# The opening of an eight-block attention and FFN kernel: statistics reordered, one head corrected on TensorE, three heads left to the quartets

## The chip, the cores and the metric

The kernel is one program on one core of a Trainium2 chip. Five engines work side by side, each on its own list of instructions in a fixed order: TensorE (PE in the profile), VectorE (DVE), ScalarE (ACT), GpSimd (POOL) and SyncE (SP), which issues DMAs. An instruction starts when its own engine has come to it and the semaphores that it names have been counted up by others. The metric is the device time of one execution in microseconds, as the median of several runs. All times below are microseconds unless marked otherwise.

## The reference, cut to what matters

The reference is a chain of eight residual blocks on an input of 2 sequences of 512 rows and 512 columns (that is what the kernel reads; it is held as eight tiles of 128 rows by 512 columns, four to a sequence). Each block takes the rows, normalises each of them, computes an attention or an FFN, and adds the result to the rows. The change touches only the first block, a latent attention with 32 heads:

```python
xn = (x - mean(x)) / sqrt(var(x) + 1e-5)        # row by row
C_q = xn @ Wq_d + bq_d                          # 12 columns
C_kv = xn @ Wkv_d + bkv_d                       # 4 columns
q = (C_q @ W_qk + b_qk)                         # 32 heads of 4 columns
scores = q . C_kv / sqrt(4)                     # per head, all pairs of rows
out = softmax(scores) @ (C_kv @ Wv_u + bv_u)    # per head
x = x + out @ Wo + bo
```

The second block (an FFN with a low-rank adapter) begins inside the first one: its preparation and products for the first sequence are interleaved with the last part of the attention. Blocks three to eight follow and are the same instructions in the same order in both kernels.

## The kernel before, in words

The function `attn_latent_small` is the first block. Products in fp32 take TensorE several passes, so queries and keys are kept as two parts, a high part rounded to a shorter format and the rest. Packed side by side along the contraction, one fast product then gives nearly the fp32 result. The helper `halved` makes them: `top` is the high part (a product with a constant column, line 481), and line 482 adds it to the full value in the packed tile. It works on VectorE for the first sequence's keys and latent queries and on POOL for everything else.

**The opening.** PE runs 30 transposes of the identity (`warm`). Meanwhile the four row tiles of the first sequence arrive by DMA. VectorE takes statistics of a tile (`statistics`, lines 205, 207, 241), POOL the inverse root (line 243), and VectorE writes the centred rows `xn` (line 215). PE transposes `xn` (`place`, line 228) and ScalarE copies the result into the room of the transposed rows. This goes by pairs: statistics of tiles 0 and 1, centring of 0 and 1, then the same for 2 and 3. After each tile come 5 or 10 more `warm` transposes. Then VectorE prepares the packed query weights `wqks` (lines 787 and 788) and takes the statistics of the second sequence's four tiles; PE computes the latent queries and the latent keys of the first sequence (line 473, 4 fp32 products each), and VectorE evicts and packs them (lines 497 and 490, 481, 482).

**Heads.** There are 8 groups of 4 heads for each sequence, called t; `head(b, t)` makes the packed queries of one. It is a fast product (line 503), and then one of two ways. For heads 0 and 1 of the first sequence, ScalarE copies the high part (line 506), PE adds a correction into the same bank (`correct`, line 199), and ScalarE copies the bank to the packed queries (line 509). For all others, ScalarE copies the bank into a buffer `wv_diag` (line 513), and POOL makes both parts (lines 481 and 482). There is one buffer `wv_diag`, so the next such copy waits for POOL; it is used later for other things as well, as is the buffer `ctxT`.

**Quartets.** A quartet u (0 to 15) is one t of one sequence. For it there are 16 score products (line 589), each reduced on VectorE to the row maximum (line 597). POOL splits the maxima (lines 606 and 607). `maxima` transposes them on PE and corrects the packed queries by them (lines 615, 199, 618). Then the transposed scores (line 627) go through ScalarE's exponential (line 630), and PE multiplies them with the latent values (line 637). The work of neighbouring quartets overlaps: the loop has eight steps per quartet, and each issues two score products of the next quartet, two transposed products of this one, and on every second step the values of an earlier one. Scores and transposed scores have three PSUM banks each, the values have bank 6, and everything else has bank 7 alone, as long as the loop runs up to the last quartet.

**What fills the gaps.** A list `extra` holds pieces of other work as generators: the remaining heads, the transposes of the second sequence (`put`), its latents (`queries(1)`, `latents(1)`), the fold of two weights into one, the bias, and later the division, projection and FFN products of the first sequence. `slices(cost)` takes pieces from the front until their costs reach the given sum (a matmul, a put or a head is 1). Twelve steps ahead of the loop (`n` from 0 to 11) each issue two scores, a slice and two filler products (`fill`, line 758) that keep PE busy. In the loop, a step takes a slice when it has no values to do; the last quartet takes more. Where `extra` is empty at the start of a slice, three fills stand there instead. In these two loops PE's instructions stay in the order in which the program issues them; the other engines' order is chosen by a scheduler. In the opening both PE and VectorE keep the program's order.

When the values of the last quartet of a group of four are done, `following(u)` gives further pieces, which are put at the end of `extra`. Behind the loop, what is left in `extra` is run.

## Time and profile before

| quantity | value |
|---|---|
| median of three runs | 1962.3 (1960.98 to 1963.4) |
| time of the profiled execution | 1963.88 |
| its span, first to last instruction | 1962.2 |
| mean granted TensorE clock | 0.997 |
| PE busy | 1930.2 (98%) |
| VectorE busy | 1373.6 (70%) |
| POOL busy | 1020.8 (52%) |
| ScalarE busy | 937.7 (48%) |
| first row tile landed | 3.42 |
| query products start | 12.12 |
| first score product | 23.36 |
| quartet loop starts | 42.04 |
| last quartet's steps start | 234.81 |
| its raw sums are transposed | 254.49 |

The span and the profiled execution's time differ by 1.7, what lies around the program. The profiled execution is 1.6 longer than the median. A PE that is busy for 98% sets the end almost everywhere, but ends of matmuls are modelled and neighbouring ones overlap, so the starts are what is read here. The rows of the first block are at the beginning; its last products are at about 262.

### The profile page before, as it was taken

What the parts mean: (1) busy time and instruction counts of PE and PEld (TensorE: products, weight loads), DVE (VectorE), ACT (ScalarE), POOL (GpSimd) and SP (SyncE); (2) the same over time, 40 slices, a digit from 0 to 9 for tenths busy, and PEclk for the clock granted to TensorE, in tenths of its full rate; (3) what the DMA queues carried; (4) which work ended last, traced back from release to release, by engine and by line L of the source; (5) the groups of instructions that cost most, each with busy time, mean ns of one, the idle gap of its engine ahead of it and who ended that gap; (6) DMA issues with size and microseconds to landing.
All of it is one profiled execution on the core that took longest, in us unless ns stands there. A gap on an engine that the chain in (4) does not pass through costs nothing.

```text
span 1962.2 us, 40652 instructions
## 1 busy us (share of the span) xinstructions
PE 1930.2 (98%) x15690; PEld 1201.3 (61%) x15690; DVE 1373.6 (70%) x3457; ACT 937.7 (48%) x2460; POOL 1020.8 (52%) x1112
## 2 busy tenths in 40 slices
PE   9999999999999999999999999999999999999999
PEld 5333356777777777777777545666565554654654
DVE  8889658767776676777765577777777755847853
ACT  3786624444444343444443167666666411641550
POOL 4331055776756667677763246565655546216221
PEclk9999999999999999999999999999999999999999
DMA  3010222322321322232223213020101002002001
GB/s 136 17 44 1 76 70 69 86 76 89 94 67 46 97 76 82 76 98 76 79 79 86 71 23 109 8 74 7 62 13 55 23 11 49 2 2 43 2 2 44
DMA packets 69296, 108.96 MB, mean 56 GB/s; under 512 B 13922, under 2 KB 48994, under 8 KB 62052
## 3 DMA queue, kind: packets, MB, share of 16 engines
q1 hardware_dynamic: 68804, 104.15, 18.2%
q8 instruction: 127, 2.08, 0.4%
q0 software_dynamic: 288, 2.10, 0.3%
q14 instruction: 77, 0.63, 0.1%
HBM read 80.00 MB, written 4.19 MB: 43 GB/s over the span
## 4 chain that ended last, share of the span: by engine, by line
PE 87%; POOL 5%; DVE 4%; issue 2%; ACT 1%; DMA 0%; SPq 0%; DVEq 0%; POOLq 0%; ACTq 0%
PE held L1022 13%; PE held L281 11%; PE held L1157 9%; PE held L190 9%; PE held L357 8%; PE held L637 3%; PE held L589 3%; PE held L1094 3%; PE held L473 2%; PE held L1516 2%; PE sc L190 2%; PE held L1513 1%; PE tp L1789 1%; PE held L1514 1%; PE sc L2109 1%
## 5 line engine op out<-in xcount | busy, mean ns | idle before, releaser
L302 ACT ACTIVATE room<-room,nmax 128x128 f32<-128x128 f32 (+3 forms) x384 | 212.6, 557 | 354.6 <-DVE nmax L292 352.4
L281 PE MATMUL held<-kT,q 128*32 128x32 f32 (+15 forms) x4096 | 264.2, 397 | 5.3 <-DVE invs L310 1.7
L292 DVE CUSTOM_DVE_ANT_0 room<-held,mask 128x128 f32<-128x128 f32 (+3 forms) x384 | 179.0, 487 | 63.3 <-PE held L281 57.9
L281 PEld LDWEIGHTS held<-kT,q 128*32 128x32 f32 x4096 | 143.4, 110 | 87.2 <-issue 38.0
L357 PE MATMUL held<-turned,vals 32*128 32x384 f32 (+7 forms) x2784 | 190.0, 416 | 0.5 <-issue 0.5
L597 DVE TENSOR_REDUCE nm<-held 128x1 f32<-128x512 f32 x256 | 161.2, 682 | 22.4 <-PE held L627 14.8
L357 PEld LDWEIGHTS held<-turned,vals 32*128 32x128 f32 (+1 forms) x2784 | 149.3, 167 | 39.2 <-issue 22.6
L315 ACT ACTIVATE room<-room,invs 128x128 f32<-128x128 f32 (+3 forms) x316 | 153.3, 551 | 41.9 <-DVE invs L310 41.7
L254 DVE TENSOR_TENSOR rows<-rows,held 128x512 f32<-128x512 f32 x198 | 129.5, 673 | 31.8 <-PE held L1022 31.3
L330 DVE STREAM_TRANSPOSE turned<-room 128x1152 f32<-128x1152 f32 x80 | 107.8, 1361 | 40.3 <-ACT room L315 21.6
L243 POOL TENSOR_TENSOR rstd<-ve,mhalf 128x1 f32<-128x1 f32 x64 | 36.2, 569 | 179.4 <-DVE ve L241 176.1
L1183 POOL TENSOR_TENSOR q<-q,room 128x256 f32<-128x256 f32 x64 | 45.3, 729 | 124.2 <-DVE q L1166 113.6
L1201 POOL TENSOR_TENSOR q<-q,cosq 128x512 f32<-128x512 f32 x60 | 88.0, 1467 | 31.6 <-DVE t L1198 31.6
L1157 PE MATMUL held<-room,w 128*128 128x256 f32 x384 | 95.0, 383 | 0.0
L1202 POOL TENSOR_TENSOR q<-q,t 128x512 f32<-128x512 f32 x64 | 86.7, 1355 | 6.3 <-DVE q L1201 2.5
L302 ACT ACTIVATE probs<-probs,nmax 128x128 f32<-128x128 f32 (+3 forms) x128 | 70.6, 553 | 37.8 <-DVE nmax L292 37.0
L1022 PE MATMUL held<-w,ctxT 128*128 128x256 f32 x360 | 86.5, 383 | 0.1
L589 PEld LDWEIGHTS held<-keys,qs 32*128 32x128 f32 x256 | 31.1, 181 | 85.4 <-DVE nm L597 58.9
L630 ACT ACTIVATE pt<-held 128x512 f32<-128x512 f32 x128 | 69.7, 599 | 26.1 <-PE held L627 20.7
L2123 POOL TENSOR_SCALAR_AFFINE_SELECT room<-room 128x512 f32<-128x512 f32 x32 | 20.3, 635 | 118.2 <-ACT room L2119 118.2
L1537 POOL TENSOR_TENSOR q<-t,t 64x512 f32<-64x512 f32 x62 | 78.9, 1272 | 4.9
L630 ACT ACTIVATE room<-held 128x512 f32<-128x512 f32 x128 | 69.6, 600 | 24.4 <-PE held L627 21.7
(441 smaller groups left out, 5005.1 us busy)
## 6 DMA issues: line engine op xcount, KB each, us to landing
w<-in_b_wq SPq DMA_DIRECT2D x16, 1024.0 KB, 4.9
w<-in_b_wo SPq DMA_DIRECT2D x16, 1024.0 KB, 5.8
vals<-v SPq DMA_DIRECT2D x256, 64.0 KB, 2.1
w<-in_m_wo SPq DMA_DIRECT2D x8, 1024.0 KB, 6.3
w<-in_b_wk SPq DMA_DIRECT2D x16, 256.0 KB, 2.8
w<-in_b_wupv SPq DMA_DIRECT2D x16, 256.0 KB, 2.6
w<-in_m_wqn SPq DMA_DIRECT2D x8, 384.0 KB, 3.6
rows<-in_x SPq DMA_DIRECT2D x8, 256.0 KB, 4.7
```

The costliest lines, as they stand in the source:

```text
L190: last = self.nc.tensor.matmul(out, lhsT, rhs, start=(i == 0), stop=(i == len(pairs) - 1))
L254: self.nc.vector.tensor_tensor(x, x, ps.rearrange("p (t d) -> p t d", t=2), op)
L281: nc.tensor.matmul(ps[32 * i : 32 * i + 32, a - lo : b - lo], q[:, at : at + 32], keys[:, a:b], start=True, stop=True,)
L292: nc.vector.tensor_tensor_reduce(out=row, in0=ps[:, :kv], in1=self.mask_back[:, :kv] if qt % 2 else self.mask[:, S - kv :], op0=ALU.add, o ...
L302: nc.scalar.activation(row, row, AF.Exp, bias=nmax, scale=-1.0, accum_out=total[:, qt : qt + 1])
L315: self.nc.scalar.activation(row, row, AF.Identity, scale=each)
L330: self.nc.vector.transpose(out[:, :last], probs[:, :last])
L357: self.nc.tensor.matmul(out[:, :, :n], values(i, j), rhs, start=(j == blocks[0]), stop=(j == stop[i]),)
L597: k.latest = nc.vector.tensor_reduce(nm[u % 2][:, qt, at : at + 1], ps, AX.X, ALU.max, negate=True).ins
L630: nc.scalar.activation(probs[u, kc][:, g], ps, AF.Exp)
L1022: k.nc.tensor.matmul(out, lhsT[:, i, bass.ts(t, P)], rhs[i], start=not (after or t or i), stop=i == 1, skip_group_check=True,)
L1157: nc.tensor.matmul(out, lhsT[:, c], rhs[:, c], start=c == 0, stop=c == 1)
```

## The change

It has five parts, all in `attn_latent_small`.

- *Row statistics in another order.* The statistics of tiles 0, 1 and 2 come first, then the centring of 0 and 1, then the statistics of 3, and the centring of 2 and 3. The transposes and `warm` products of PE keep their order. Of the second sequence's four statistics, the last stands behind the packing of the latent queries.
- *One head corrected on TensorE.* Only head 0 is made by correction, and it is made at once: its product, five transposes of the identity, the correction, five transposes, then two fills ahead of the first scores. Before, heads 0 and 1 were made with two fills, two corrections and four fills. The high part of the first sequence's keys (`latents(0)`) goes to the buffer `wv_diag` instead of the two buffers `high`.
- *Two buffers for the query products.* Odd t use `ctxT`, even t `wv_diag`. The tile of `halved` is kept to one buffer for tags other than `high`. The weights' fold, which writes `ctxT`, is made later by the scheduler.
- *Three heads left.* Heads 5, 6 and 7 of the first sequence leave the twelve steps and stand at the head of the loop's list; head 1 comes into the twelve steps. The steps 10 and 11 then find `extra` empty and take three fills each. Heads 5 to 7 count as light pieces (`light`), as the second sequence's heads do.
- *The division earlier.* For the first half of a sequence (`half == 0`), `following(u)`, which is one division, goes to the second place of `extra` instead of to its end.

By the built programs' order, PE gets ten more transposes and two more fills and loses one correction; VectorE's instructions are the same in number. The last pieces shift: the last quartet takes three more products of the FFN and no division of quartet 11, and one put and one centring stand behind the loop.

```diff
-            top = lp.tile(list(out.shape), F32R, tag=tag, name="high")
+            top = lp.tile(list(out.shape), F32R, tag=tag, name="high", bufs=1 if tag != "high" else None)
...
-            k.latest = halved(nc.gpsimd if b else nc.vector, keys[b], full, 0)
+            k.latest = halved(nc.gpsimd if b else nc.vector, keys[b], full, 0, "high" if b else "wv_diag")
...
-            if (b, t) < (0, 2):
+            if (b, t) == (0, 0):
...
-            full = one([P, S], "wv_diag")
+            full = one([P, S], "ctxT" if t % 2 else "wv_diag")
...
-                extra.extend(following(u))
+                at = len(extra) if half else 1
+                extra[at:at] = following(u)
...
-            for t in range(0, NT, 2):
-                pair = [k.statistics(t + i) for i in range(2)]
-                centred = [k.centred(t + i, known=pair[i]) for i in range(2)]
-                for i in range(2):
-                    k.place(t + i, centred[i], k.turn)
-                    k.warm(5 + 5 * i)
+            ahead = [k.statistics(t) for t in range(3)]
+            centred = [k.centred(t, known=ahead[t]) for t in range(2)]
+            ahead.append(k.statistics(3))
+            for t in range(NT):
+                if t == 2:
+                    centred += [k.centred(i, known=ahead[i]) for i in (2, 3)]
+                k.place(t, centred[t], k.turn)
+                k.warm(10 if t % 2 else 5)
...
-            known = {t: k.statistics(t) for t in range(NT, NTILES)}
-            run([queries(0), latents(0)])
+            known = {t: k.statistics(t) for t in range(NT, NTILES - 1)}
+            run([queries(0)])
+            known[NTILES - 1] = k.statistics(NTILES - 1)
+            run([latents(0)])
             first = k.latest
-            starts = [head(0, t) for t in range(2)]
-            for _ in range(3):
-                for piece in starts:
-                    next(piece, None)
-                fill(2, of_values)
-        extra = [centre(NT, NT + 1), head(0, 2), head(0, 3), put(NT), put(NT + 1)]
+            for _ in head(0, 0):
+                k.warm(5)
+            fill(2, of_values)
+        extra = [centre(NT, NT + 1), head(0, 1), head(0, 2), head(0, 3), put(NT), put(NT + 1)]
         extra += [centre(NT + 2, NT + 3), latent_values(0), head(0, 4), put(NT + 2)]
-        extra += [put(NT + 3), head(0, 5), head(0, 6), head(0, 7)]
-
+        extra += [put(NT + 3)]
+
+        others = [head(0, t) for t in range(5, 8)]
...
-        later = [queries(1), latents(1), *heads[:4], latent_values(1)]
+        later = [*others, queries(1), latents(1), *heads[:4], latent_values(1)]
...
-                    light = not extra or extra[0] in heads + adds
+                    light = not extra or extra[0] in others + heads + adds
```

## The prediction

> **What bounds the kernel.** I read the page first, then a table of stretches of the first stage, then the engines' rows in order of time and the chain inside it. Everything below is in the first 262 us: behind the last transposes of this stage the order of instructions on all five engines is the same in both kernels, so the other 1,700 us are taken as unchanged.
>
> The page of the profiled execution, span and busy shares:
> ```profile
> span 1962.2 us, 40652 instructions
> ...
> PE 1930.2 (98%) x15690; PEld 1201.3 (61%) x15690; DVE 1373.6 (70%) x3457; ACT 937.7 (48%) x2460; POOL 1020.8 (52%) x1112
> ```
> PE is hardly ever idle. So a matmul added costs its length, unless it falls into one of PE's waits; the waits are what has to be found. The stretches of the first stage (columns: length, then busy time and instructions of PE, weight load, DVE, ACT, POOL, the granted clock, DMA):
> ```profile
> 0.00:21.34 21.34, 17.68 (x95) 13.19 (x95) 15.44 (x37) 4.28 (x7) 10.35 (x25) 1.00 0.80 273
> 21.34:42.04 20.70, 20.14 (x87) 11.30 (x87) 18.09 (x39) 7.37 (x13) 10.03 (x12) 1.00 0.12 41
> 42.04:48.17 6.13, 6.13 (x25) 2.12 (x25) 5.45 (x10) 4.63 (x9) 2.25 (x3) 1.00 0.00 0
> ...
> 139.06:172.23 33.17, 31.54 (x195) 11.25 (x195) 30.96 (x57) 23.34 (x44) 4.86 (x9) 1.00 0.00 1
> ...
> 210.81:234.81 24.00, 24.00 (x139) 7.80 (x136) 16.09 (x28) 17.56 (x33) 1.42 (x5) 1.00 0.08 31
> 234.81:254.49 19.68, 18.97 (x94) 6.52 (x93) 7.60 (x17) 10.38 (x20) 1.65 (x3) 1.00 0.16 54
> ```
> The opening (to 21.34) has 3.7 us of PE idle, the last quartets (210.81 to 254.49) almost none: what moves there costs its full length. Four steps after 42.04 are PE's too. The chain of waits through the opening:
> ```profile
> 12.28 6.88 PE held L473 x16
> ...
> 20.50 0.70 DVE keys L482
> ...
> 21.34 0.71 PE held L758 x2
> 22.04 0.47 PE held L199 x2
> 22.51 0.92 PE held L758 x4
> 23.43 0.42 PE held L589
> ```
> Query and latent products, then the keys' two halves on DVE, then fills and corrections, then the first scores. VectorE's rows ahead of that, and the loads of row tiles 1 and 2 (SyncE, line 90):
> ```profile
> 5.46 0.54 DVE L215 TENSOR_SCALAR xn<-rows,ln_mv,rstd 128x512 f32<-128x512 f32 x1
> 6.45 0.55 DVE L215 TENSOR_SCALAR xn<-rows,ln_mv,rstd 128x512 f32<-128x512 f32 x1 [0.45 <-POOL rstd L243]
> 6.91 0.69 DVE L205 BATCH_NORM_STATS2 ln_stats<-rows 128x6 f32<-128x512 f32 x1
> ```
> ```profile
> L90 SPq DMA_DIRECT2D rows<-in_x x2: 417/424/432, 1.3 to 1.7; - x2
> ...
> DMA to landing us min/median/max: 3.0/3.7/4.4
> ```
> The second of these two loads is tile 2: issued at 1.7, landed 4.4 later, at about 6.13. Before, its statistics are asked for only at 6.91, so nobody waits.
>
> **The change, part by part.**
>
> *Row statistics.* Tile 2's statistics now stand ahead of the first centring in VectorE's order. They start at 6.15 (landing) instead of the centring's 5.46. One group (3.44 to 4.46) takes 1.02 in period, so xn0 starts at 7.16, ends at 7.71, and PE's first transposes start at 7.75, not 6.40. The wait for the square root (0.45) is filled, but it was not on PE's path. PE then has two rounds of 4 transposes, 5 warm ones, 4, 10, each 9.54 to 12.12 = 2.58 long: 7.75 + 5.16 = 12.91 for the query products, against 12.12. The later centrings are in time: xn1 8.2 for 8.7, xn2 9.6 for 10.3, xn3 (root at 10.05) 10.6 for 11.3. Cost +0.79. If the tile had landed by 5.46 it would be +0.1; if PE's clock falls in the wait, see the rivals.
>
> *One statistic moved behind the query product.* VectorE idles 0.84 before the latents' eviction (19.19), later 19.98; the group of 1.0 ends by about 19.5. Nothing; without that cover up to 0.5.
>
> *One head corrected on TensorE, its fills.* The keys follow the latents by the same 2.15, so the first fill starts at 21.34 + 0.79 = 22.13. From there to the first score stood two fills, two corrections, four fills (21.34 to 23.36, 2.02); two fills remain (0.54): first score 22.67. The single head's product, ten transposes (10 x 0.109; the chain has ten in 1.09), its correction and copies (0.59 each) run while PE would wait for the keys: the copy ends at 20.80, the last transposes by 21.6, before 22.13. The own buffer for the keys' high part ends a wait of ScalarE (1.3) that was beside. Gain 1.48 against 0.79: the scores start 0.69 earlier.
>
> *Twelve score steps.* Steps 0 to 8 hold the same four heads, four puts and latent values as before, in another order; head 1 with its two POOL operations (0.69 + 1.28) has the second buffer. Steps 9 to 11 lose two heads (0.43 each in the chain, at 23.86) and get six fills (0.235 each, by the chain's pairs of 0.47). Before, 37.68 to 42.04 = 4.36 was 3.56 of PE and 0.8 waits for VectorE (eight reductions of 0.61 and the coefficients). Now PE has 3 x 0.43 + 12 x 0.235 = 4.11; VectorE ends about then. I take 4.2, -0.15 (bounds -0.25 and +0.55: all hidden, none hidden). The quartet loop starts 0.84 earlier.
>
> *Three heads in the loop.* They take the first three slots, where fp32 products of 1.06 stood. A slot's head shares one bank (7) with the next, so the next product waits for ScalarE's copy, which queues behind two exponentials:
> ```profile
> L630 ACT ACTIVATE room<-held 128x512 f32<-128x512 f32 x128 | 69.6, 600 | 24.4 <-PE held L627 21.7 <-PE held L589 1.9
> ...
> L513 ACT COPY wv_diag<-held 128x512 f32<-128x512 f32 x14 | 8.3, 593 | 10.1 <-POOL qs L482 6.0 <-PE held L503 4.1
> ```
> In order of time two exponentials take 1.09 (not 2 x 0.6), so a step is 1.09 + 0.59 = 1.68 of ScalarE, against 0.86 of PE. Four steps: 0.62 to the first exponential, 3 x 1.68, 0.1, one product 1.06 = 6.82, against 6.13: +0.69. Bounds: PE alone 7 x 0.43 + 1.06 = 4.07 (-2.06), POOL's 2.05 per head 3 x 2.05 + 1.49 = 7.64 (+1.51). I take ScalarE's, since the four pairs of steps with a head from 91.02 to 102.10 last 2.77 each = 4 x 0.545 + 0.59, ScalarE's sum. The second buffer gives nothing there: of the 6.0 above, 5.6 lie in the opening, 0.4 in the loop.
>
> *The shift.* Every later piece comes three slots later. Slots are fixed in number, a heavy pair of steps lasts 2.93. Three query products come in at 2.93, three products of tile 1 leave for the last quartet at 2.92; the division of quartet 11 moves up (2.80) into the place of the one empty slot (141.07 to 143.92, 2.85). Sum 0, bounds -1.0 and +1.0: the 1.6 of PE idle in 139 to 172, where VectorE has 30.96 of 33.17.
>
> *The last quartet.* It takes three more products of 1.06 and loses a division's and a put's transposes (0.59 each): +2.0, PE is full there. The put now stands behind the loop, in PE's 0.71 wait for the copy of the raw sums: 0. The last centring is ready 4.7 us after the last step's start, its transposes are due at 5.2: no wait. Bounds +1.4 (half a product hidden) and +2.6 (put not covered).
>
> Sum: -0.69 - 0.15 + 0.69 + 0 + 2.0 = **+1.85 us**. A check by work: PE gets ten transposes (1.09) and two fills (0.47), loses a correction (0.24), +1.3; the rest is 2.8 more idle in the first steps less what the waits near 20, 40, 141 and 254 us give up.
>
> The profiled execution took 1963.88 us with a span of 1962.2; the median of three is 1962.3. On its own time the sum gives 1965.7; on the median **1964.1 us**, +0.09%. A measurement of this kernel tells about 0.2% (3.9 us) from no change, so this is no change.
>
> **The clock, row and rule.** PE is now idle from 6.4 to 7.75. The granted clock by stretches of 3.4 us:
> ```profile
> 18.44:21.85 3.41, 1.69 (x6) 0.86 (x5) 2.59 (x5) 1.15 (x2) 0.00 (x0) 1.00 0.93 378
> 1800.20:1803.60 3.40, 1.95 (x17) 1.23 (x16) 1.96 (x9) 0.00 (x0) 3.32 (x3) 1.00 0.63 104
> 1803.60:1807.00 3.40, 3.40 (x8) 1.18 (x4) 2.75 (x9) 0.00 (x0) 0.26 (x1) 0.50 0.46 75
> ```
> With 1.69 of PE busy in such a stretch the clock stayed, with 1.95 it was halved for the next. The stretch 4.78 to 8.20 will have about 2.1. So the rows allow either; halved, 3.41 us do half their work, 1.7 lost. [...]
>
> **The rivals.**
> - *The third tile decides (slower).* PE's idle grows with tile 2's landing; from 6.55 on (0.4 later than here) PE has about 1.7 or less in its stretch and I would expect the halved clock: 0.4 + 1.7 above my sum, 1966.2 and more. For it: the 4.4 us from issue to landing against 2.6 for tile 0. Against: the row at 18.44. The halved clock without a later landing gives 1965.8.
> - *The heads hide (faster than my sum).* If ScalarE's copies do not hold up PE, the first steps cost 4.07: -2.75, 1961.3. For it: ACT is busy 48%. Against: the single bank.
> - *The order of statistics does what it says.* Tile 2 landed by 5.46: 1963.4. Against: the landing row.
> - *A gain that shows* (under 1958.4) would need the heads hidden and the last quartet free as well: 1964.1 - 2.75 - 2.0 = 1959.3 is not there yet, and with the middle's -1.0 it just is.
>
> **Numbers.** My sum, with the order-of-statistics case, 0.59; the third tile and the clock 0.19, nearly all beyond 3.9 us or close below it; heads hidden 0.16; all hidden at once 0.05; not thought of 0.01. Faster by over 0.2%: 0.06; slower by over 0.2%: 0.18; same 0.76. Range: from 1960.0 (heads hidden and half the middle's bound) to 1967.0 (the third tile a little later still).
>
> **What would show it.** Right: VectorE's third statistics wait for a load at 5.5 to 6.1; the query products start at 12.9; first score 22.7; loop start 41.2; ScalarE without idle in the three following steps; 11 products of 1.06 in the last quartet. Wrong: a clock of 0.5 in 8.2 to 11.6; PE stalls at the maxima, because POOL's splits now stand behind other waiting operations of its queue; VectorE's reductions waiting between 139 and 172.

## The result, and the profile after

| | kernel before | changed kernel |
|---|---|---|
| median of 20 executions each, same chip | 1963.70 | 1968.68 |
| lowest and highest | 1960.68, 1966.06 | 1964.13, 1970.80 |
| profiled execution, its span | 1962.2 | 1968.7 |

The ratio is 1.0020 with a 95% interval of 1.0014 to 1.0026: the change makes the kernel 2.7 to 5.1 us slower. It goes by mean times, about 1967.8 against 1963.6; the median of the changed kernel lies 0.9 above its mean. The prediction said +1.85 us on 1962.3, thus 1964.1, and 1960.0 to 1967.0. So the sign of the sum was right and its size was not, and the base was too low as well: the median of three executions shown before was 1962.3, that of the 126 executions of the kernel before that came with all later runs is 1964.1.

The page of the changed kernel, span and busy shares:

```profile
span 1968.7 us, 40679 instructions
...
PE 1933.3 (98%) x15701; PEld 1203.2 (61%) x15701; DVE 1375.7 (70%) x3457; ACT 937.0 (48%) x2459; POOL 1022.3 (52%) x1114
```

PE has 3 us more to do, and the span is 6.5 longer. The stretches of the first stage (length, then busy time and instructions of PE, weight load, DVE, ACT, POOL, then the granted clock, the DMA share and GB/s): up to the first filler, up to the loop's start, the first four steps, the rest of quartet 0, and then four stretches of 3.41 us as the clock is granted:

```profile
0.00:22.09 22.09, 18.82 (x105) 14.19 (x105) 15.83 (x37) 4.80 (x7) 9.78 (x25) 1.00 0.78 268
22.09:41.87 19.78, 19.35 (x85) 10.92 (x85) 17.76 (x39) 5.28 (x9) 8.28 (x10) 1.00 0.12 38
41.87:49.08 7.21, 6.29 (x22) 2.27 (x21) 5.12 (x9) 5.64 (x11) 4.70 (x6) 0.74 0.00 0
49.08:57.16 8.08, 8.08 (x43) 2.50 (x43) 4.82 (x8) 4.62 (x9) 1.50 (x3) 0.81 0.01 2
38.57:41.98 3.41, 3.41 (x18) 2.01 (x16) 2.90 (x6) 0.00 (x0) 0.00 (x0) 1.00 0.00 0
41.98:45.39 3.41, 2.66 (x14) 1.08 (x14) 2.83 (x5) 2.92 (x7) 1.18 (x2) 1.00 0.00 0
45.39:48.81 3.42, 3.25 (x7) 1.08 (x7) 2.23 (x4) 2.72 (x6) 3.34 (x4) 0.50 0.00 0
48.81:52.22 3.41, 3.41 (x17) 0.79 (x16) 1.29 (x2) 1.08 (x2) 1.69 (x4) 0.50 0.02 5
```

The clock is halved from 45.4 to 52.2, two stretches, directly behind the stretch with 2.66 of 3.41 us busy. That is where the three heads stand. Quartet 0 (41.88 to 57.16 by its transposed scores) takes 15.28 us instead of 12.82.

The same milestones in both profiles show where the difference comes and goes:

| milestone | before | after | difference |
|---|---|---|---|
| query products | 12.12 | 12.87 | +0.75 |
| first score product | 23.36 | 22.72 | -0.64 |
| step 9 of twelve | 37.68 | 37.03 | -0.65 |
| loop, first score product | 42.04 | 41.87 | -0.17 |
| loop, first transposed product | 42.22 | 41.88 | -0.34 |
| quartet 1 | 55.04 | 57.16 | +2.12 |
| quartet 6 | 117.47 | 120.59 | +3.13 |
| quartet 15 | 234.81 | 237.74 | +2.93 |
| copy of the last centred rows (ScalarE) | 255.62 | 260.35 | +4.74 |
| a copy of the context (ScalarE) in the third stage | 1302.39 | 1308.91 | +6.52 |

Behind the first block two things differ that no instruction of the change causes by its work. Up to 1169 the difference falls to 3.27; 1.0 of this falls between 1162 and 1169, just behind a halved stretch that the profiled execution of the kernel before has (from 1158.5) and that of the changed kernel has not. Then it rises to 6.52, and 2.8 of this rise is two waits of PE for nothing that the profile shows. Its waits between 1160 and 1320 in the changed kernel (engine and line, releaser, total, times, longest):

```profile
PE held L357 <- issue: 2.8, 2, 1.4
```

In the kernel before this row is missing in that stretch. From 262 to 1800 it has 0.5 us of such waits at this line. This is taken up at the end.

### The profile page after: what moved, and what is told of

Same layout as the page of the kernel before. It is cut to its first block, busy times and chain, and to the rows that moved or that the text cites. A ratio compares the mean times of both kernels' runs of the same rounds, so it can differ in the third digit from the quotient of the medians.

```text
span 1968.7 us, 40679 instructions
## 1 busy us (share of the span) xinstructions
PE 1933.3 (98%) x15701; PEld 1203.2 (61%) x15701; DVE 1375.7 (70%) x3457; ACT 937.0 (48%) x2459; POOL 1022.3 (52%) x1114
## 4 chain that ended last, share of the span: by engine, by line
PE 86%; POOL 5%; DVE 4%; issue 2%; ACT 1%; SPq 1%; DMA 0%; POOLq 0%; DVEq 0%; ACTq 0%
PE held L1026 13%; PE held L281 11%; PE held L1161 9%; PE held L190 9%; PE held L357 8%; PE held L637 3%; PE held L1098 3%; PE held L589 2%; PE held L473 2%; PE sc L190 2%; PE held L1520 2%; PE held L1517 1%; PE tp L1793 1%; PE held L1518 1%; PE pj L190 1%
```

## The experiments

All runs set a kernel beside executions of the kernel before on the same chip. Since single executions of one kernel spread widely (the 126 of the kernel before over 8.9 us), two more numbers are given: the **clock's loss**, which is one minus the granted clock (as recorded, to three places) times the span, averaged over the executions, and the time **at full clock**, the mean time less that loss. Over the 126 executions of the kernel before, time rises by 0.83 us for each us of this loss, over the 20 of the changed kernel by 0.84: the loss explains most of the spread, and slightly overstates its cost, or is blurred by the rounding.

| kernel | executions | ratio, 95% interval | clock's loss | at full clock |
|---|---|---|---|---|
| before | 126 | 1 | 5.4 ± 0.2 | 1958.7 |
| changed | 20 | 1.0020 (1.0014, 1.0026) | 6.8 ± 0.6 | 1961.0 |
| before_again | 12 | 1.0003 (0.9994, 1.0012) | 5.9 | 1958.5 |
| fills_in_waits | 11 | 1.0013 (1.0005, 1.0022) | 5.2 | 1961.2 |
| heads_early | 12 | 1.0023 (1.0014, 1.0031) | 8.0 | 1960.4 |
| pairs_order | 11 | 1.0016 (1.0007, 1.0024) | 6.1 | 1961.1 |
| heads_early_apart | 12 | 0.9993 (0.9985, 1.0002) | 4.6 | 1959.3 |
| pairs_heads_apart | 11 | 0.9984 (0.9976, 0.9993) | 3.0 | 1958.9 |
| before_heads_left | 7 | 1.0036 (1.0025, 1.0047) | 9.0 | 1963.1 |
| before_two_buffers | 11 | 1.0007 (0.9999, 1.0016) | 6.3 | 1959.1 |
| after_apart | 5 | 1.0037 (1.0024, 1.0051) | 9.1 | 1962.2 |
| no_three_fills | 11 | 1.0012 (1.0003, 1.0022) | 6.8 | 1959.5 |
| before_statistics | 11 | 1.0006 (0.9997, 1.0015) | 5.9 | 1959.0 |
| single_head | 11 | 0.9999 (0.9990, 1.0008) | 6.1 | 1957.8 |
| fills_moved | 11 | 1.0012 (1.0003, 1.0022) | 4.6 | 1961.3 |
| heads_early_filled | 11 | 1.0017 (1.0008, 1.0026) | 7.0 | 1960.0 |
| single_head_again | 11 | 0.9997 (0.9988, 1.0006) | 5.2 | 1957.8 |
| pairs_heads_apart_again | 11 | 0.9997 (0.9988, 1.0006) | 4.8 | 1958.5 |

The loss of a kernel with 11 executions has a standard error of about 0.6 (0.4 to 0.9).

### The kernel before once more

No edit.

> The kernel before itself, to learn how many stretches of halved TensorE clock its executions have. In the profile of the changed kernel the clock is halved from 45.4 to 52.2 us, two stretches of 3.413 us, right behind the three steps with a head; the kernel before had none in its first 1,150 us. Theory A (the halved clock behind these steps makes the larger part of the loss): the executions of the kernel before have one to two halved stretches fewer in the mean than those of the changed kernel, that is a mean clock of about 0.998 where the changed kernel has 0.9965 in the mean (one stretch is 0.5 x 3.413 / 1965 = 0.0009), and nothing halved before 1,150 us. Theory B (shift of the slots and last quartet alone; the halved stretches come by chance in any kernel): the same mean clock in both. Ratio 1.000 in either.

Measured: a ratio of 1.0003, a mean clock of 0.9970 where the changed kernel has 0.9966. The profiled execution has one halved stretch before 1,150 us, at 175. The mean clocks therefore lie closer than theory A wanted: the changed kernel loses 1.4 ± 0.6 us more, less than one stretch (1.7) in the mean, not one to two.

This profile also shows something about the opening. PE's rows:

```profile
1.47 6.42 PE L86 MATMUL held<-ident 128*128 128x128 f32 x30 [1.47 <-POOL ident masks.py:199]
7.73 0.60 PE L228 MATMUL held<-ident,xn 128*128 128x128 f32 x4
```

The 30 identity transposes took 6.42 us here and 5.09 in the first profile. The clock was full only from 7.52 on; in the first profile it was from 4.78, and there the transposes start 0.213 us apart up to 4.72 and 0.109 apart from 4.87 on. The transposes of the rows start at 7.73 for that reason alone, although the centred rows are there at 6.03.

### Fillers in the three waits

```diff
+                        if u == 0 and 1 <= step <= 3:
+                            fill(2, of_values)
                         slices(2 if u == last else 1)
```

> The changed kernel with two fillers put into PE's three waits for ScalarE's copies, ahead of the slice in the steps 1, 2 and 3 of the loop (0.44, 0.48 and 0.51 us of idle PE; two fillers take 0.47 to 0.66). Nothing else moves. Theory A: no halved clock between 42 and 56 us, the step 4 starts 6.3 to 6.7 us after step 0 (7.2 in the changed kernel), quartet 1 begins 2 us earlier, and the median falls from 1968.7 by 1.5 to 3 us, to 1966 to 1967 beside a kernel before of 1963.7 (ratio 1.0015). Theory B: the fillers cost up to 0.6 us and nothing is given back, ratio 1.0025 to 1.003.

Measured: 1.0013 instead of 1.0020, loss 5.2. The stretches of this kernel: the first four steps, and the two clock stretches that answer to those above:

```profile
41.32:47.53 6.21, 6.21 (x29) 2.82 (x29) 5.10 (x9) 5.50 (x11) 3.79 (x4) 1.00 0.01 3
42.73:46.14 3.41, 3.41 (x18) 1.74 (x19) 3.07 (x6) 3.41 (x8) 2.48 (x3) 1.00 0.00 0
46.14:49.55 3.41, 3.41 (x21) 1.08 (x21) 2.46 (x5) 2.35 (x6) 3.24 (x4) 1.00 0.03 5
```

PE is never idle, ScalarE fills its 3.41 us as the prediction's sum for ScalarE had it, and the clock stays at 1.00. The four steps take 6.21 us, the kernel before 6.13; quartet 0 takes 12.87 (before 12.82, changed 15.28). PE's rows of steps 1 and 2, the fillers of line 759 between the transposed scores and the head's product:

```profile
42.59 0.49 PE L627 MATMUL held<-qm,keys 32*128 32x512 f32 x2
43.02 0.74 PE L759 MATMUL held<-keys,unit 128*128 128x512 f32 x2
43.59 0.44 PE L503 MATMUL held<-cq,wqks 128*128 128x512 f32 x1
43.96 0.50 PE L589 MATMUL held<-keys,qs 32*128 32x512 f32 x2
```

Compare the changed kernel's rows at the same place:

```profile
43.15 0.49 PE L627 MATMUL held<-qm,keys 32*128 32x512 f32 x2
44.08 0.49 PE L503 MATMUL held<-cq,wqks 128*128 128x512 f32 x1 [0.44 <-ACT ctxT L513]
44.51 0.50 PE L589 MATMUL held<-keys,qs 32*128 32x512 f32 x2
...
45.55 0.79 PE L503 MATMUL held<-cq,wqks 128*128 128x512 f32 x1 [0.48 <-ACT wv_diag L513]
```

Theory A holds for this place: with the fillers the clock stays full. The fillers do two things at once, though. They take away the idle time, and they put products with all 128 rows between products of which 12 of 14 (in the changed kernel's stretch from 41.98) have 32 rows. Which of the two keeps the clock, no run separates. In this execution the first block ends 1.80 us behind the kernel before instead of 4.74, and 0.54 of this difference is its earlier opening.

### The heads back in the twelve steps

```diff
-        extra += [put(NT + 3)]
-        others = [head(0, t) for t in range(5, 8)]
+        extra += [put(NT + 3), head(0, 5), head(0, 6), head(0, 7)]
+        others = []
```

> The changed kernel with the heads 5, 6 and 7 back in the twelve steps; all else stays changed. The loop then begins with fp32 products as in the kernel before, no three fillers stand in the steps 10 and 11, and the last quartet has eight products and its division again. Theory A: no halved clock near 45 us (-2 to -2.5), last quartet -1.8, the steps 10 and 11 -0.5, the rest of the shift -0.8 to 0: a median about 0.6 us below the kernel before (the scores start 0.64 us earlier there): ratio 0.9995 to 1.000. Theory B: only the work of the shift and the last quartet comes back (-2.6 of the 5): ratio 1.001 to 1.0015. Theory C (the order of the row statistics, with PE idle from 6.4 to 7.8 us, is what costs, through the clock): ratio 1.002 as now.

Measured: 1.0023, which no theory except C had. The expected gain in the first steps is there (quartet 1 begins 0.62 ahead of the kernel before), but quartet 5 takes 2.3 us more. Of this, 0.9 is not the wait shown here: quartet 5 takes 13.19 in pairs_heads_apart and 12.31 in single_head, which differ in the division's place alone. The rest is in these rows:

```profile
105.97 1.27 POOL L482 TENSOR_TENSOR qs<-ctxT,high 128x512 fp32r<-128x512 f32 x1
107.28 0.69 DVE L542 TENSOR_TENSOR ctxT<-c_own,a_wvT 128x512 f32<-128x512 f32 x1 [0.15 <-POOL qs L482]
108.02 0.30 PEld L473 LDWEIGHTS held<-w,ctxT 128*128 128x128 f32 x2 [1.80 <-DVE ctxT L542]
```

That wait is a cost of the two buffers. `ctxT` is the buffer into which the fold writes (line 542). In the kernel before the fold is written at 22.0 and lies ready. Now the odd heads of both sequences use `ctxT`, the last of them until 107.24, so the fold is written just ahead of the product that needs it, and PE waits. The changed kernel has the same wait, 0.6 us long, in the last step of quartet 5 (at 119.56).

### The row statistics by pairs

```diff
-            ahead = [k.statistics(t) for t in range(3)]
...
+            for t in range(0, NT, 2):
+                pair = [k.statistics(t + i) for i in range(2)]
+                centred = [k.centred(t + i, known=pair[i]) for i in range(2)]
...
```

> The changed kernel with the row statistics by pairs again (statistics 0 and 1, centring 0 and 1, then 2 and 3); all else stays changed. Theories A and B: PE's first transposes at 6.4 instead of 7.8 us, query products 0.75 us earlier, first score at 21.95, and 0.75 us less in all: ratio 1.0017 where the changed kernel has 1.0020 to 1.0025. Theory C: 3 us less and fewer halved stretches, ratio 1.0005.

Measured: 1.0016 and no other loss of the clock than the changed kernel's within its error. Query products at 12.14 against 12.87, first score at 21.98. The gain of 0.73 there is the one that was expected. Theory C falls here.

### The heads early, and the fold left alone

```diff
-            full = one([P, S], "ctxT" if t % 2 else "wv_diag")
+            full = one([P, S], "ctxT" if t % 2 and b == 0 else "wv_diag")
```

on top of heads_early.

> heads_early with one thing more: only the first sequence's odd heads use the buffer ctxT, the second sequence's heads use wv_diag as in the kernel before. The fold of two weights, which writes ctxT on VectorE (line 542) and is then multiplied on PE, no longer has to wait for the last head's POOL operations. In the profile of heads_early PE stood 1.32 us for that at 106.7 to 108.0 and quartet 5 lost 2.2 us; the executions of heads_early lost 8.0 us in the mean to the halved clock (one minus the granted clock, times the span), those of the kernel before 5.2, and at full clock they would take 1960.4 against 1958.7. Theory F (the fold's wait is a cost of the two buffers, and its idle PE lets the clock be halved in some executions): no wait for line 542, 1.3 to 2 us less at full clock (1958.3 to 1959.1), the clock's loss falls to 5 to 6.3, ratio 0.9995 to 1.0007. Rival C (idle PE in the opening halves the clock, or the loss sits in the last quartets): the clock's loss stays at 7.5 to 8.5, ratio 1.0012 to 1.0018.

Measured: 0.9993 where heads_early has 1.0023. The row of PE waiting for line 542 is gone, the loss is 4.6 instead of 8.0. One line of the change, the buffer's name for the second sequence's heads, costs 0.0030 of 1964 us, 5.9 us with an error of about 2.5 (both intervals are ± 0.0009), when everything else is as here. The visible wait is 1.3 us; how it comes to more in the mean is asked once more below.

### The same with the statistics by pairs

> heads_early_apart with the row statistics by pairs again: of the change, the single head corrected on TensorE with its fills and two buffers in the first sequence stay. Theory F with the opening as read: first score at 21.95, 1.4 us ahead of the kernel before where the full clock starts in the same place, nothing given back later: 0.3 to 0.75 us less than heads_early_apart, ratio 0.9992 to 1.0000 against the kernel before. Rival (an earlier start is swallowed by the next waits for ScalarE and VectorE, as between the steps 0 and 1 of heads_early, 2.04 us instead of 1.5): ratio 0.9998 to 1.0008.

Measured: 0.9984 (0.9976, 0.9993), first score at 22.00. Compared with heads_early_apart the opening gives 1.0 us, and this set had the lowest loss of all, 3.0.

### Three heads left to the loop, alone

```diff
-        extra += [put(NT + 3), head(0, 5), head(0, 6), head(0, 7)]
+        extra += [put(NT + 3)]
+        others = [head(0, t) for t in range(5, 8)]
...
-        later = [queries(1), latents(1), *heads[:4], latent_values(1)]
+        later = [*others, queries(1), latents(1), *heads[:4], latent_values(1)]
...
-                extra.extend(following(u))
+                at = len(extra) if half else 1
+                extra[at:at] = following(u)
```

on the kernel before.

> The kernel before with this part of the change alone: the heads 5, 6 and 7 stand at the head of the loop's list, and the division stands at the second place of the list, without which the three slots' delay would leave the raw sums' buffer waiting for itself. One buffer for the query products, old order of the statistics, old opening. The three steps wait for POOL as well (2.0 us per head). Theory A (three heads in the loop cost by the halved clock behind them, by three products in the last quartet, and by fillers): the clock halved from about 45 to 52 us in executions whose windows fall so, a clock's loss of 6.2 to 7.5 us in the mean against 5.2, last quartet +1.8, 2.3 to 4 us more at full clock (1961 to 1962.7), ratio 1.002 to 1.003. Rival (the heads are nearly free; the loss is that of the two buffers' fold and of the order of statistics): ratio 1.000 to 1.0008.

Measured: 1.0036, the worst but one. The clock is halved for three stretches from 47.4 on, loss 9.0, and 4.4 us at full clock. So this part, with the division's place that goes with it, is the costly one, and the second buffer of the query products, which the prediction had given no worth in the loop, saves it from more: with one buffer ScalarE's copies wait for POOL, and PE for them. The waits of PE in the loop:

```profile
PE held L503 <- ACT wv_diag L513: 2.2, 2, 1.8
PE held L589 <- DVE nm L597: 1.9, 5, 0.5
PE held L473 <- ACT wv_diag L513: 1.2, 1, 1.2
```

The changed kernel has the second of these rows as well; in place of the first it has 0.5 + 0.4, and the third is missing there.

### Two buffers, alone

```diff
-            full = one([P, S], "wv_diag")
+            full = one([P, S], "ctxT" if t % 2 else "wv_diag")
```

on the kernel before.

> The kernel before with the two buffers for the query products alone (odd heads through ctxT, even ones through wv_diag, in both sequences). Theory F: the fold's multiplication moves from 22.0 us to behind the last head, PE waits 0.6 to 1.3 us for it once between 105 and 125 us, and some executions get a halved stretch there: 0.6 to 2 us more at full clock, ratio 1.0005 to 1.002. Rival: the scheduler hides it, and the copies that no longer wait for POOL give a little: ratio 0.9995 to 1.0003.

Measured: 1.0007 (0.9999, 1.0016). The fold is now written at 103.90, PE idles 0.83 ahead of the product at 104.72, and the rows, 0.1 to 0.2 later than in the kernel before up to there, are 0.5 to 0.6 later from there to the end of the block. At full clock +0.4. The direction is theory F's, but the interval does not exclude nothing.

### The heads left, and the fold left alone

The line of heads_early_apart, on the changed kernel.

> The changed kernel with the second sequence's heads back in one buffer (only the first sequence's odd heads use ctxT), so that the fold has nothing to wait for. Against heads_early_apart it differs by one thing: the heads 5, 6 and 7 are left to the loop. Theory A: the three heads cost 1.8 us in the last quartet, 0.5 in the steps 10 and 11 and about as much in the first steps at full clock (1961 to 1962 where heads_early_apart has 1959.3; the changed kernel 1961.0, of which the fold's wait of 0.6 goes), and their idle PE another halved stretch in the mean, a clock's loss of 6 to 7 us against 4.6: ratio 1.0012 to 1.0020. Theory F alone (the fold's wait makes the halved stretches of the changed kernel as it does in heads_early): loss 4.6, ratio 1.0003 to 1.0010.

Measured: 1.0037 in five executions, worse than the changed kernel, which neither theory had. The fold now waits in a worse place. VectorE's rows:

```profile
50.17 0.69 DVE L542 TENSOR_TENSOR ctxT<-c_own,a_wvT 128x512 f32<-128x512 f32 x1 [2.44 <-POOL qs L482]
50.78 2.48 DVE L597 TENSOR_REDUCE nm<-held 128x1 f32<-128x512 f32 x4
```

The last user of `ctxT` is head 7, whose POOL work ends at 50.1 because it is one of the three that came late. VectorE has the fold next in its order, stands 2.44 us, and four reductions queue behind it; the score products wait for them (1.59 at 51.51), and the clock is halved from 51.4 to 58.2. In the changed kernel as it is, the fold comes after the second sequence's heads, and this stall does not exist. So a buffer that two pieces share costs where its last user comes late, whichever that is.

### Without the three fillers

```diff
-            if not extra:
-                fill(3, k.ring[-1])
```

> The changed kernel without the three fillers that stand in each of the steps 10 and 11 where the list is empty. The steps took 1.98 and 1.77 us with five fillers; with two they should take 1.33 or VectorE's two reductions, 1.3. If the fillers are the mis-sized term: the loop starts 0.9 to 1.1 us earlier and that stays, 1960.0 at full clock. They also keep PE busy ahead of the three steps with a head: without them the stretch of 3.4 us that holds the steps 10 and 11 has about 0.35 us idle more and the clock may be halved in more executions, a loss of 7 to 9 us against 6.8. Ratio 1.0015 if only the first holds, 1.0020 to 1.0030 if both.

Measured: 1.0012, loss 6.8 as the changed kernel's, at full clock 1959.5. Rows of PE: the changed kernel first, then this one.

```profile
37.46 0.73 PE L759 MATMUL held<-keys,unit 128*128 128x512 f32 x2
38.12 0.69 PE L589 MATMUL held<-keys,qs 32*128 32x512 f32 x2
38.74 1.43 PE L759 MATMUL held<-keys,unit 128*128 128x512 f32 x5
40.10 0.49 PE L589 MATMUL held<-keys,qs 32*128 32x512 f32 x2
40.52 1.42 PE L759 MATMUL held<-keys,unit 128*128 128x512 f32 x5
41.87 0.49 PE L589 MATMUL held<-keys,qs 32*128 32x512 f32 x2
```

```profile
37.91 0.68 PE L589 MATMUL held<-keys,qs 32*128 32x512 f32 x2
38.52 0.73 PE L759 MATMUL held<-keys,unit 128*128 128x512 f32 x2
39.19 0.74 PE L589 MATMUL held<-keys,qs 32*128 32x512 f32 x2
39.86 0.73 PE L759 MATMUL held<-keys,unit 128*128 128x512 f32 x2
40.52 0.61 PE L589 MATMUL held<-keys,qs 32*128 32x512 f32 x2
```

The steps 10 and 11 take 1.98 and 1.77 us with five fillers, 1.28 and 1.33 with two. The six fillers cost 1.1 us, and the halved stretches behind the heads are there in either case (43.1 to 50.0 here).

### The new order of the statistics, alone

The lines of the change that begin with `ahead`, on the kernel before.

> The kernel before with the new order of the row statistics alone. Where PE's first transposes start depends on two things: on the centred rows (6.4 us by pairs, 7.2 to 7.8 in the new order, with tile 2 landed between 5.6 and 6.4) and on the identity transposes ahead of them, which run at half clock until the clock is first full, at 4.3 us in one profile and at 7.5 in another; with the late one the kernel before itself starts them at 7.73. So the new order costs 0.75 us where the clock is full early and about nothing where it is late: 0.2 to 0.6 us in the mean at full clock, with no more halved stretches (5.2 to 6.3 us of loss, as the kernel before): ratio 1.0001 to 1.0005. Theory C (1.4 us of idle PE ahead of the first transposes makes the clock fall): loss above 6.5, ratio 1.0008 or more.

Measured: 1.0006 (0.9997, 1.0015). In the profiled execution 0.74 us from the query products to the end of the block, with no change on the way. The clock's loss, 5.9 ± 0.4, is that of the kernel before within the errors. This speaks against theory C a second time, although the interval of the ratio still holds its 1.0008.

### One head corrected on TensorE, nearly alone

pairs_heads_apart with `extra.extend(following(u))` as before.

> pairs_heads_apart with the division at the end of the list again: of the change are left the one head corrected on TensorE with its fillers, the last statistic behind the query product, and two buffers in the first sequence. Opening 1.36 us earlier than the kernel before (first score at 22.0). In pairs_heads_apart 0.9 us of 1.5 were lost between quartets 5 and 8, where the division stood in another place; if that is the division's place, it stays here and at full clock the time is 1957.3 to 1958.2 against 1958.7 of the kernel before; ratio 0.9982 to 0.9993, depending on the halved stretches, 3 to 5.2 us. If the wins of the opening are swallowed later in any case: 0.9995 to 1.0003.

Measured: 0.9999. The loop starts 1.5 us early, loses 0.56 in its first step (step 0 takes 2.04 instead of 1.48) and 0.2 more in the same quartet, and 0.70 stay, the same number in every quartet to the end of the block, so the opening's gain is not swallowed further on. At full clock 1957.8, 0.9 under the kernel before. It does not show in the ratio.

### The fillers moved

fills_in_waits without the three fillers of the steps 10 and 11.

> The changed kernel with its fillers moved: none in the steps 10 and 11 where the list is empty, and two in each of PE's three waits behind the steps with a head. Theory A: the loop starts 1.2 us earlier as without the fillers (40.6), no clock is halved between 42 and 56 us, 1959.5 to 1960.3 at full clock (fills_in_waits 1961.2, no_three_fills 1959.5), a clock's loss as in the kernel before, 5.2 to 5.6 us: ratio 1.0004 to 1.0010. What stays is the last quartet. If the halved stretches behind the heads do not come from that idle PE: a halved clock near 45 us, a loss of 6.8, ratio 1.0012 to 1.0018.

Measured: 1.0012, loss 4.6, no halved clock before 1199.8. Quartet 0 takes 12.85, the first block ends 1.43 behind the kernel before, against 1.80 with the fillers left in. The clock part came out as expected. The time at full clock, 1961.3, is a good 1 us more than expected; of this the profiled execution shows 2.3 us of PE's waits for nothing visible, 1.8 more than the kernel before has, and the rest stays open.

### Fillers ahead of the fold

```diff
             yield 0
+            fill(5, k.ring[-1])
             ps = k.turn()
```

in the fold, on top of heads_early.

> heads_early with five fillers (1.2 us) ahead of the fold's product, in PE's wait of 1.32 us for the fold's multiplication. If that idle time lets the clock be halved in other executions than the profiled one: the wait is covered, the time at full clock stays at 1960.3 to 1960.7, and the clock's loss falls from 8.0 to 5 to 6.3 us, ratio 1.0008 to 1.0015. If the clock's loss of heads_early has another cause: loss 7.5 or more, ratio 1.0020 to 1.0026.

Measured: 1.0017, loss 7.0 ± 0.6 against 8.0 ± 0.6. PE's idle time ahead of the fold's product is filled, from 106.69 to 108.08, and the loss does not fall clearly. So it is not shown that this idle time halves the clock. Why heads_early loses so much clock stays open.

### The two twins once more, side by side

> The same kernel as single_head (one head corrected on TensorE, last statistic behind the query product, two buffers in the first sequence), beside its twin on the same chip. It was 0.9 us under the kernel before at full clock with a clock's loss 0.8 us larger, ratio 0.9999. If the loss is chance, it is 0.9992 to 0.9998 now; if this opening brings halved stretches of its own, 0.9998 to 1.0003.

> The same kernel as pairs_heads_apart, beside its twin on the same chip: it differs from single_head in the division's place alone. Its ratio of 0.9984 went with a clock's loss of 3.0 us, 2.6 less than the kernel before, and no gain at full clock. If the earlier division really saves halved stretches (by work in the one empty slot near 142 us, for one): again a loss of 3 to 4 us and a ratio of 0.998 to 0.999. If that was chance: a loss of 5 to 6 us, ratio 0.9995 to 1.0002.

Measured: 0.9997 for both, with intervals of ± 0.0009. The low loss of 3.0 did not come back (4.8), so the 0.9984 was in part chance. Both sets of each kernel together, 22 executions: a mean of 1963.4 for single_head and 1962.6 for pairs_heads_apart, the kernel before 1964.0. Something of the change, the one head corrected on TensorE with two buffers in the first sequence, is 0.6 to 1.4 us to the good, 0.03 to 0.07%, and no run settles that it is more than noise. Nothing tried beats the kernel before clearly.

### All profiles together

| | halved clock between 42 and 58 us |
|---|---|
| the three heads in the loop, their waits empty: changed, pairs_order, before_heads_left, after_apart, no_three_fills | in 5 of 5 profiles, from 43.1 to 51.4 on, for two or three stretches (in after_apart behind VectorE's stall) |
| the three heads in the loop, their waits filled: fills_in_waits, fills_moved | in 0 of 2 |
| no head in the loop's first steps: all others, with the first profile of before | in 0 of 11 |

The executions say the same, more weakly: a loss of 6.5 ± 0.4 in the changed kernel and pairs_order (31), 4.9 ± 0.4 with the waits filled (22), 5.4 ± 0.2 in the kernel before. The difference is about one stretch in the mean, while each profile has two or three: not every execution has them. Where in the program an execution lost its clock, only a profile tells; heads_early loses 8.0 without a halved stretch in the first block of its profile, so a difference in the loss alone does not point at the loop.

## Why the prediction was wrong

**The base.** The sum was put on a median of three. It was 1.4 us under the median of 20 and 1.8 under that of 126. Of the 4.6 us between 1964.1 and 1968.7, about 1.8 is this. By a line through the executions (time against the clock's loss), the changed kernel is 2.5 us behind at no loss of clock, 0.6 more than the 1.85 of the sum, and 1.2 more for the clock (1.4 us of loss at 0.84); 0.9 is the distance of its median from its mean.

**Three heads in the loop** is the step that failed: "so a step is 1.09 + 0.59 = 1.68 of ScalarE", "Four steps: 0.62 to the first exponential, 3 x 1.68, 0.1, one product 1.06 = 6.82, against 6.13: +0.69". The order of events was right: PE's product waits for ScalarE's copy in bank 7, ScalarE has no pause. The size was not. Two exponentials and a copy follow one another at 1.43, since each starts before the end of the one ahead (in the changed kernel the exponentials from 42.47 to 43.56, the copy at 43.44, the next exponentials at 43.91, the next copy at 44.87), and with the waits filled the four steps cost 0.08 more than before, not 0.69. What the step lacked is the clock, which was put at no cost behind these waits. The prediction did ask this question, but at another place: it watched the single wait of 1.4 us in the opening ("Wrong: a clock of 0.5 in 8.2 to 11.6"), where no profile of the 18 has a halved clock, and never applied it to the three waits that its own sum had just put into the loop. Measured: +2.46 in the profile from the loop's start to quartet 1, where the text had +0.69; with the waits filled +0.04.

The row that it set against its first rival, "With 1.69 of PE busy in such a stretch the clock stayed", does not settle the matter: here 2.66 busy of 3.41 and no gap above 0.48 were followed by a halved clock. Nor do the number and the length of the waits order the rows. In no_three_fills the clock is halved at 43.13 behind a stretch with a single wait, of 0.48. A single wait of 1.80 at one and the same place was followed by a halved clock in single_head and not in fills_in_waits, and in the changed kernel a stretch without any wait was followed by one. Three pairs of stretches, of fills_in_waits, single_head and the changed kernel (columns as above):

```profile
1155.47:1158.89 3.42, 1.62 (x25) 0.70 (x16) 3.01 (x14) 3.14 (x10) 1.62 (x3) 1.00 0.00 0
1158.89:1162.30 3.41, 3.07 (x39) 1.76 (x40) 3.41 (x10) 0.83 (x4) 1.81 (x4) 1.00 0.19 39
...
1154.14:1157.55 3.41, 1.61 (x26) 0.68 (x19) 3.21 (x13) 2.58 (x10) 0.44 (x1) 1.00 0.06 13
1157.55:1160.96 3.41, 3.08 (x19) 1.31 (x18) 2.97 (x11) 1.40 (x6) 2.96 (x5) 0.50 0.18 37
...
1827.15:1830.57 3.42, 3.42 (x20) 1.91 (x18) 3.42 (x14) 1.64 (x3) 0.00 (x0) 1.00 0.00 0
1830.57:1833.98 3.41, 3.41 (x24) 3.15 (x22) 2.59 (x12) 1.85 (x4) 0.64 (x1) 0.50 0.02 5
```

**Twelve steps**, "-0.15 (bounds -0.25 and +0.55: all hidden, none hidden)": measured +0.48 (4.84 instead of 4.36, from step 9 to the loop), just inside the upper bound. The term was 3 x 0.43 + 12 x 0.235. A filler costs 0.235 only behind another filler (0.228 to 0.236 from start to start at 39.08 to 39.78 of the changed kernel). The first behind a pair of scores takes 0.33 to the next filler, and the last 0.32 to 0.33 until the next pair. A pair with five fillers is thus 1.77, not 1.6, three pairs cost 0.5 more, and one pair waited 0.19 more for VectorE. The chain of the kernel before, where two fillers stand at 0.47, did not show this, because there a head's product (0.33 to 0.34 behind the pair) paid for the change of kind.

**The shift**, "Sum 0, bounds -1.0 and +1.0": measured +0.81 from quartet 1 to quartet 15, within the bounds. There is a wait of 0.6 in it that the text does not have, for the fold's buffer. That the fold "is made later by the scheduler" stood in the description of the change, and the prediction did not ask who waits for it. before_two_buffers and heads_early show such waits too, 0.8 and 1.3 us in their profiles. It does not explain the +0.81, though: after_apart has no such wait between these quartets and still loses 0.59 there. The rest stays open.

**What was right.** Row statistics, +0.79: tile 2's statistics started at 6.19 upon landing, xn0 at 7.20, transposes at 7.79, query products 0.75 later. The cost depends on when the clock is first full, though: where that is late, the identity transposes end late and hide it (in before_again, full from 7.52, the transposes start at 7.73 with the old order, in the changed kernel, full from 4.43, at 7.79). One head and its fills, -1.48: first filler at 22.09 (22.13 in the text), first score at 22.72 (22.67). The last quartet, +2.0: measured +1.81 from quartet 15's start to the copy behind it; since heads_early, without the three heads, has +0.45 there as well, their part is nearer to 1.4. The rows of VectorE's third statistics that wait for a load:

```profile
6.19 0.69 DVE L205 BATCH_NORM_STATS2 ln_stats<-rows 128x6 f32<-128x512 f32 x1 [0.60 <-DMA rows<-in_x]
...
7.20 0.99 DVE L215 TENSOR_SCALAR xn<-rows,ln_mv,rstd 128x512 f32<-128x512 f32 x2
...
7.79 0.66 PE L228 MATMUL held<-ident,xn 128*128 128x128 f32 x4 [1.41 <-DVE xn L215]
```

**The sum at full clock** came out in one profile: fills_in_waits, which has no halved stretch in the block, ends it at +1.80, and the text said +1.85. That is luck in good part: its query products started 0.54 us earlier than in the changed kernel's profile, because tile 2 landed earlier, and misses of opposite sign cancel (the twelve steps cost 0.6 more than the text had, the shift 0.8 more, the first steps with filled waits 0.6 less).

**The rivals.** A halved clock without a later landing had the right mechanism in the wrong place, and its price of 1.7 a stretch was a little high: one stretch at 175 cost 1.43 in before_again. "The third tile decides" fell: tile 2 landed at 6.19, where the text had 6.13, and the opening kept its clock. "The heads hide" fell as well: ScalarE's copies do hold up PE, 0.44 and 0.48 in the rows above, and even with the waits filled the four steps took 6.21, where this rival had 4.07. "The order of statistics does what it says" fell: tile 2 landed at 6.19 here, and at 5.64 to 6.46 in the other profiles with the new order.

## What to carry to other kernels

Moving a piece of work into a slot is more than the difference of the lengths: list the waits that it opens on PE, one by one, and ask at each of them what the clock will do, the short ones included; fillers placed exactly in those waits, ahead of the product that waits, cost 0.08 us in the four steps here, and the clock stayed full in both profiles with them. When a piece takes over another's buffer, look for the next writer of this buffer on every engine and for what is queued behind it. And take the base of a sum from as many executions as there are: here the median of three was 1.4 to 1.8 us off, about as much as the whole sum of +1.85.

## What had not been expected of the hardware

- *Where the clock's stretches begin differs from one execution to the next.* The clock was first full at 4.3 to 7.5 us of the span in the 18 profiles, and all halved stretches lie on a grid of 3.413 us from there (in the changed kernel full at 4.43, halved at 45.40, twelve times 3.413 behind it). The same kernel starts its first useful transposes at 6.40 or 7.73 for that.
- *PE waits of up to 1.7 us for nothing visible* (1.7 in fills_moved), in the dense products of line 357. In the changed kernel they are 1.43 and 1.41 us, ahead of the products that stand 6,485 and 5,342 from the end. Total behind the first block: 0.5 us in both profiles of the kernel before, 2.8 in the changed kernel, 0.6 and 1.4 in the two profiles of pairs_heads_apart. In the changed kernel a packet of 16,384 bytes on an instruction queue starts at 1199.83 and takes 0.94, the wait lasts from 1200.7 to 1202.1, the next such packet starts at 1203.54. Whether PE waited for its instructions is not shown.
- *What decides on the clock is not the busy share as the profile models it*: 1.69 of 3.41 us kept it, 1.95 and 2.66 did not. In the 18 profiles the clock falls to half 55 times behind a stretch at full clock, ends of the program left out, and in 23 of these stretches PE is busy for at least 3.3 of the 3.41 us. All 23 hold products of 32 rows for the larger part, at most four with 128 rows and 128 columns. One of them in the kernel before ends at 1895.77 with 3.40 busy, one in the changed kernel at 1830.57 with 3.41. What sets these stretches apart from others as busy is not shown.
